# Twenty-one transposes of a fused attention and MLP kernel taken from TensorE to a trip of 32 by 32 blocks through DRAM and VectorE

## The chip, the cores and the metric

The kernel runs on one core of a Trainium2 chip. The metric is device microseconds of one execution; the time before is the median of three. An execution has five instruction streams: TensorE (PE, with its weight loads shown apart as PEld), VectorE (DVE), ScalarE (ACT), GpSimd (POOL) and SyncE (SP). In this kernel SP issues every DMA, in the order of the program. Each engine works off its own stream in order, and a semaphore holds an instruction until what it reads is there.

## The reference, cut to what matters

The input is `x`, four sequences of 512 tokens with 512 features, all float32. A gated linear attention and then an MLP with 4-bit weights are each added to the residual:

```python
x = x + attention(layernorm(x))
x = x + down(gelu(gate(layernorm(x))) * up(layernorm(x)))
```

The attention works by head (4 of 128 features) and by chunk (4 of 128 tokens in each sequence):

```python
q, k, v = h @ Wq + bq, h @ Wk + bk, h @ Wv + bv       # h = layernorm(x)
k = k / max(norm(k), 1e-12)
scores = (q @ k.T) * beta.T * decay                    # within a chunk, causal
y = scores @ v + (q @ state) * chunk_decay
state = state * total_decay + v.T @ (k * beta * decay_to_end)
```

A product on TensorE contracts over partitions. So `h`, which is computed with tokens on partitions, has to be turned until features lie on partitions before it can be multiplied with a weight, and `k` has to be turned the same way before `q @ k.T`.

## The kernel before, in words

**Units of work.** A norm tile is 128 tokens of one sequence with all 512 features; sequence `b` has four, `n` = 0 to 3. Its turned form goes into `hT[b]`, two tiles of 128 partitions. A chunk `(b, n)` is the attention of 128 tokens of sequence `b`.

**Steps.** The kernel is recorded by hand (`manual_schedule`), so each engine's order is the order in which the Python code issues. The main loop counts steps `p`; sequence `b` has the twelve steps 12b to 12b+11: four products `product_v` (L375, L382), four `product_q` (L400), four `product_k` (L412). After each product `behind(p)` issues the rest of the step. The chunks of sequence `b` run nine steps behind: chunk `(b, n)` takes the three steps from p = 9 + 12b + 3n. A period here is such three steps:

- `p % 3 == 0`: `chunk_lead` (L519) turns `k` by four transposes on TensorE, and ScalarE copies the result into `kT` (L522). `chunk_decay` makes the decay `dm` on ScalarE (L534) and GpSimd (L538).
- `p % 3 == 1`: `turn("f")` transposes the MLP's norm tile (L333, `tp_f`). ScalarE rounds it to `g` (L356), VectorE forms two more parts (L357, L358), and three DMAs store them (L360). `turn("a")` transposes the attention's next norm tile (L333, `tp_a`), and ScalarE copies it to `hT` in two parts (L348). Then `chunk_scores`: TensorE forms `sp` (L586), and VectorE multiplies it into `dm` (L597).
- `p % 3 == 2`: `chunk_sums`: TensorE forms `dp` (L611) and `yp`, which reads `dm` (L640, L642). VectorE adds `yp` to the residual `xr` (L649), and SP stores it (L650). Then `second_norm` takes the statistics of `xr`, `first_norm` those of the next sequence's tile (L298 to L305), and `settle` normalises both (L312: first `hn_f`, then `hn_a`).

So from one `yp` on VectorE to the next there is a cycle: `xr`, both norms, `settle`, then the `g` parts and `dm`, then the next `yp`.

**When norm tiles come.** `early` in the code sets it: sequence 1 at p = 2, 5, 8 and 8; sequence 2 at p = 11, 14, 17, 20; sequence 3 at p = 23, 26, 29, 32. Sequence 0 is turned at the start.

**Other work in the same streams.** At `j` = 3 to 7 of each sequence the gates are computed: `gates_ln` (p % 12 == 5) is a chain of small VectorE operations with two ScalarE logarithms in the middle (L467 to L482). Unpacking of MLP weights is slipped in between (L162 to L183), and `fetch` issues the loads of the next weights (L196, L201 for `gu`, six DMAs; L215, L217 for `d`, two DMAs). Loads of the MLP's first inputs (L283, `x<-h`) begin at p = 40.

**Buffers.** Tiles of 2 KB per partition come from a list of 42 free places (`one_k`), PSUM from eight banks in turn. DMAs use eight semaphores in turn, so a DMA waits until the one issued eight places earlier has landed.

Of the kernel before, what the change touches and what calls it, by code (L numbers as in the profile page):

```python
# [8 lines left out]
F32 = mybir.dt.float32  # L9
# [4 lines left out]
AF = mybir.ActivationFunctionType  # L14
ALU = mybir.AluOpType
# [6 lines left out]
P = 128  # L22
# [13 lines left out]
def f32(t):  # L36
    return t.bitcast(F32)
# [3 lines left out]
def tile_gated_linear_attention__then__nvfp4_geglu(  # L41
# [19 lines left out]
    nc = tc.nc  # L61
    B, T, D = x.shape
    H = D // P
    NCH = T // P
    NT = B * NCH
    KC = D // P
# [8 lines left out]
    dram = ctx.enter_context(tc.tile_pool(name="dram", bufs=1, space=DRAM))  # L75
# [45 lines left out]
    one_k = Homes("b", 42, [P, T], two_k)  # L121

    def psum(name):
        return fps.tile([P, T], F32, tag="p", name=name)

    def heads(t):
        return t.rearrange("p (h d) -> p h d", d=P)

    def bc(a):
        return a.unsqueeze(2).to_broadcast([P, a.shape[1], P])  # L130
# [144 lines left out]
    acc, hT, q_sb, k_sb, v_sb = {}, {}, {}, {}, {}  # L275
# [5 lines left out]
    def load(src, name):  # L281
        t = one_k.get(name)
        nc.sync.dma_start(f32(t), src)  # L283
        return t
# [7 lines left out]

    settled, turned = [], []

    def norm(src, key, use, parts=1, within=None):

        st = small.tile([P, 6], F32, tag="st", name=f"st_{key}")
        nc.vector.bn_stats(st, f32(src))  # L298
        if within:
            within()  # L300
        mv = small.tile([P, 2], F32, tag="mv", name=f"mv_{key}")
        nc.vector.bn_aggr(mv, st)
        rs = small.tile([P, 1], F32, tag="rs", name=f"rs_{key}")
        nc.vector.tensor_scalar(rs, mv[:, 1:2], 1e-5, None, ALU.add)
        nc.gpsimd.tensor_tensor(rs, rs, minus_half[:, :1], ALU.pow)  # L305

        def settle():

            hn = one_k.get(f"hn_{key}")
            w = D // parts  # L310
            for cols in (slice(i * w, (i + 1) * w) for i in range(parts)):
                nc.vector.tensor_scalar(  # L312
                    f32(hn)[:, cols].rearrange("p (c two j) -> p c two j", two=2, j=P),
                    f32(src)[:, cols].rearrange("p (c j two) -> p c two j", two=2, j=P),
                    mv[:, 0:1], rs, ALU.subtract, ALU.mult,
                )
            one_k.put(src)
            turned.append((hn, key, use))

        settled.append(settle)  # L320
# [6 lines left out]
    def turn(which, most=NT):  # L327
        for done in [t for t in turned if t[1][0] in which][:most]:
            turned.remove(done)
            hn, key, use = done  # L330
            tp = psum(f"tp_{key}")
            for k in range(KC):
                nc.tensor.transpose(tp[:, k * P : (k + 1) * P], f32(hn)[:, k * P : (k + 1) * P], ident)  # L333
            one_k.put(hn)
            use(tp)

    def first_norm(b, n, src, within=None):
        if n == 0:
            hT[b] = [two_k.get(f"hT{b}_{c}") for c in range(KC // 2)]

        soon = b == n == 0

        def use(tp):
            for c in range(KC // 2):
                to = f32(hT[b][c])[:, :, n * P : (n + 1) * P]
                new = tp[:, 2 * c * P : 2 * (c + 1) * P].rearrange("p (two t) -> p two t", two=2)
                for part in ((0, 1), (1, 2)) if soon else ((0, 2),):
                    nc.scalar.copy(to[:, slice(*part), :], new[:, slice(*part), :])  # L348

        norm(src, f"a{b}_{n}", use, 2 if soon else 1, within)  # L350

    def second_norm(b, n, src):
        def use(tp):
# [40 lines left out]
    def product_q(b, h):  # L394
# [10 lines left out]
            f32(q_sb[b][h // 2])[:, h % 2, :], pq, AF.Identity, bias=bq_sb[:, h : h + 1]  # L405
        )

    def product_k(b, n):

        pk = psum(f"pk_{b}_{n}")  # L410
        for k in range(KC):
            nc.tensor.matmul(  # L412
                pk, f32(hT[b][k // 2])[:, k % 2, n * P : (n + 1) * P], f32(wk[k // 2])[:, k % 2, :],
                start=(k == 0), stop=(k == KC - 1),
            )
        kt = one_k.get(f"k_{b}_{n}")
        k_sb[b, n] = kt
        nc.vector.tensor_tensor(f32(kt), pk, f32(bk_sb), ALU.add)
        return lambda: k_factors(b, n, kt)

    def k_factors(b, n, kt):
        sq = one_k.get(f"sq_{b}_{n}")
        sn = small.tile([P, H], F32, tag="ss", name=f"ss{b}_{n}")
        for h in range(H):
            hs = slice(h * P, (h + 1) * P)
            nc.scalar.activation(
                f32(sq)[:, hs], f32(kt)[:, hs], AF.Square, accum_out=sn[:, h : h + 1]
            )
        one_k.put(sq)
        nc.gpsimd.tensor_scalar(sn, sn, 1e-24, None, ALU.max)  # L430
        nc.gpsimd.tensor_tensor(sn, sn, minus_half, ALU.pow)
        brn = small.tile([P, H], F32, tag="brn", name=f"brn{b}_{n}")
        nc.gpsimd.tensor_tensor(brn, sn, beta[b][:, n * H : (n + 1) * H], ALU.mult)
        kwf = small.tile([P, H], F32, tag="kwf", name=f"kwf{b}_{n}")
        nc.gpsimd.tensor_tensor(kwf, sn, bdte[b][:, n * H : (n + 1) * H], ALU.mult)
        ss[b, n] = brn, kwf
# [66 lines left out]
    def gates_end(b):  # L503
        nc.vector.tensor_tensor(bdte[b], bdte[b], beta[b], ALU.mult)
# [8 lines left out]
    state, ch = {}, {}  # L513

    def chunk_lead(b, n):
        kT = one_k.get(f"kT_{b}_{n}")
        tp = psum(f"tpk_{b}_{n}")
        for h in range(H):
            nc.tensor.transpose(  # L519
                tp[:, h * P : (h + 1) * P], f32(k_sb[b, n])[:, h * P : (h + 1) * P], ident  # L520
            )
        nc.scalar.copy(f32(kT), tp)  # L522
        ch["kT"] = kT
# [38 lines left out]
    def chunk_values(b, n):  # L562

        brn, kwf = ss.pop((b, n))
        kt = k_sb[b, n]
        if n + 1 < NCH:
            kw = one_k.get(f"kw_{b}_{n}")
            nc.gpsimd.tensor_tensor(heads(f32(kw)), heads(f32(kt)), bc(kwf), ALU.mult)
            ch["kw"] = kw
        vb = one_k.get(f"vb_{b}_{n}")  # L570
        ch["vb"] = vb
        if b < B - 1:
            nc.gpsimd.tensor_tensor(heads(f32(vb)), heads(f32(v_sb[b, n])), bc(brn), ALU.mult)
        else:
            for h in range(H):
                hs = slice(h * P, (h + 1) * P)
                nc.scalar.activation(
                    f32(vb)[:, hs], f32(v_sb[b, n])[:, hs], AF.Copy, scale=brn[:, h : h + 1]
                )
# [83 lines left out]
    for b in range(1, B):  # L663
        for n in range(NCH):
            p = 3 * NCH * (b - 1) + 3 * n - 1 if b > 1 else 2 + 3 * min(n, 2)
# [5 lines left out]
    def chunk_of(p):  # L671
        b, n = divmod((p - 2 * NCH - 1) // 3, NCH)
        return (b, n) if 0 <= b < B else None
# [24 lines left out]
    def behind(p):  # L698
        place[0] = p + 1
        b, j = divmod(p, 3 * NCH)  # L700
        chunk = chunk_of(p)
        first = b < B
        if not first:
            between_steps(p)
        left = chunk if p not in met else None
        if p % 3 == 0:
            if left:
                chunk_lead(*chunk)
            exps = gates_exp(b) if first and j == 3 else None
            if chunk and chunk[1] == 0:  # L710
                chunk_values(*chunk)
            if first and j == 6:
                exps = gates_sums(b)
            if left:
                chunk_decay(*chunk)
            if exps:
                exps()
        elif p % 3 == 1:
            turn("f")

            if p > 1:
                turn("a")
            if left:
                chunk_scores(*chunk)
            if first and j == 7:
                gates_end(b)
                load_sums(b, 0)
            for t in early.get(p + 4, ()):
                if t[0] > 1:
                    xs[t] = load(tile_of(t[0] * NCH + t[1]), f"x{t[0]}_{t[1]}")  # L730
            t = (p - 2 * NCH - 2) // 3 + 1
            if 0 <= t < NT:
                acc[divmod(t, NCH)] = load(tile_of(t), f"xr{t}")
        else:
            if first and j == 5:
                gates_ln(b)
            if chunk and not summed:
                sums, rest = chunk_sums(*chunk)
                sums()
                summed.append(rest)  # L740
            while summed:
                summed.pop()()
            for t in early.get(p, ()):
                first_norm(*t, xs.pop(t))
            if p + 1 < 3 * NCH * B:
                settle()
# [173 lines left out]
    with tc.manual_schedule():  # L920
# [3 lines left out]
        bv_sb, bk_sb = one_k.get("bv"), one_k.get("bk")  # L924
# [40 lines left out]
        blocks = mlp()  # L965
        p = 0
# [95 lines left out]
```

## Time and profile before

| | |
|---|---|
| median of three runs | 1308.07 us (1307.88 to 1308.34) |
| profiled execution, its own time | 1308.09 us |
| its span, from first to last instruction | 1306.1 us |
| the time around the span | 1.99 us |
| granted TensorE clock | 0.999 |

| stage, us from the span's start | PE busy | DVE busy | ACT busy | DMA share |
|---|---|---|---|---|
| 8.0 to 34.5 | 26.50 | 10.63 | 6.39 | 0.51 |
| 34.5 to 57.0 | 22.50 | 7.94 | 10.93 | 0.35 |
| 57.0 to 117.0 (steps 12 to 23) | 60.00 | 38.80 | 25.21 | 0.44 |
| 117.0 to 177.0 (steps 24 to 35) | 60.00 | 41.04 | 25.85 | 0.45 |
| 177.0 to 237.0 (from step 36) | 60.00 | 35.83 | 26.47 | 0.55 |
| 237.0 to 280.0 | 40.32 | 34.37 | 28.50 | 0.96 |
| 280.0 to 330.0 | 50.00 | 41.38 | 18.03 | 0.77 |

The page of a profile gives the share of busy time by engine, the chain of work that ended last (followed back from the end, with its share by engine and line) and groups of equal instructions with the mean time of one. The trace behind it can be asked for the chain in order of time, for a timeline of one engine, for the waits of one engine, and for the traffic in a short window. In a timeline the columns are start, duration, engine, line, operation and tiles; "SPq" rows are DMA issues, and their duration is the time that SP takes to issue.

### The profile page before, as it was taken

The page shows a single profiled execution, that of the slowest core. Times are in us where ns is not written, and L with a number is a line of the kernel's source. Part 1 is how long each engine was busy: PE and PEld are TensorE (multiplying, and loading weights), DVE is VectorE, ACT ScalarE, POOL GpSimd, SP SyncE. Part 2 cuts the span into 40 slices and gives each one's busy share as a digit, 9 for nine tenths or more (in the row PEclk, how much of TensorE's full clock was granted, in tenths as well). Part 3 has the DMA queues.
Part 4 walks back from the last instruction along what each step waited for, and adds up shares of the span by engine and source line. Part 5 has one row for each costly group of instructions (what it writes and reads, how often), then busy time and mean ns, then how long its engine had stood idle before and what let it go on. Part 6 is the DMA issues. An engine that isn't in the chain of part 4 may idle for free.

```text
span 1306.1 us, 17024 instructions
## 1 busy us (share of the span) xinstructions
PE 1296.4 (99%) x5808; PEld 1038.3 (79%) x5808; DVE 954.0 (73%) x1539; ACT 461.5 (35%) x908; POOL 108.9 (8%) x179
## 2 busy tenths in 40 slices
PE   9999999999999999999999999999999999999998
PEld 6677676778888888888888888888888888887886
DVE  3467665798777777777777777777777777777566
ACT  2443435753333333333333333333333333332332
POOL 1535263410000000000000000000000000000000
PEclk9999999999999999999999999999999999999999
DMA  5235446888555555555555555555555555555463
GB/s 194 82 108 173 123 128 211 266 272 261 184 184 187 187 185 183 187 186 184 185 186 186 186 187 184 186 184 187 183 186 186 188 183 186 185 177 197 169 248 128
DMA packets 176374, 240.79 MB, mean 184 GB/s; under 512 B 16096, under 2 KB 74784, under 8 KB 176288
## 3 DMA queue, kind: packets, MB, share of 16 engines
q1 hardware_dynamic: 176288, 239.72, 56.7%
q8 instruction: 45, 0.74, 0.2%
q14 instruction: 41, 0.34, 0.1%
HBM read 187.19 MB, written 52.46 MB: 183 GB/s over the span
## 4 chain that ended last, share of the span: by engine, by line
PE 96%; DMA 2%; DVE 2%; ACT 1%; issue 0%; SPq 0%; POOL 0%; DVEq 0%; ACTq 0%; POOLq 0%
PE pa L774 35%; PE p_d L818 26%; PE pb L774 17%; PE pq L400 4%; PE pk L412 4%; PE pva L375 2%; PE pvb L382 2%; PE sp L586 1%; PE yp L640 1%; PE dp L611 1%; DMA x<-h 1%; PE yp L642 1%; PE tp_a L333 1%; PE tp_f L333 0%; PE tpk L519 0%; DMA h<-g 0%
## 5 line engine op out<-in xcount | busy, mean ns | idle before, releaser
L774 PE MATMUL pa<-x,wgu 128*128 128x512 f32 x2048 | 507.1, 390 | 0.0
L774 PEld LDWEIGHTS pa<-x,wgu 128*128 128x128 f32 x2048 | 383.9, 188 | 79.0
L818 PE MATMUL p_d<-wd,i 128*128 128x512 f32 x1542 | 357.3, 390 | 2.3 <-DVE xr L649 0.6
L818 PEld LDWEIGHTS p_d<-wd,i 128*128 128x128 f32 x1542 | 288.4, 188 | 65.7 <-DVE i L798 2.1
L779 ACT ACTIVATE t<-pb 128x512 f32<-128x512 f32 x256 | 151.2, 591 | 358.9 <-PE pb L774 355.5
L774 PE MATMUL pb<-x,wgu 128*128 128x512 f32 x1024 | 275.3, 390 | 1.5 <-DMA x<-h 1.4
L780 DVE TENSOR_TENSOR t<-pa,t 128x512 f32<-128x512 f32 x256 | 176.5, 690 | 82.6 <-ACT t L779 76.9
L774 PEld LDWEIGHTS pb<-x,wgu 128*128 128x128 f32 x1024 | 192.3, 188 | 43.0 <-DMA x<-h 3.2
L826 DVE SCALAR_TENSOR_TENSOR acc<-p_d,acc 128x512 f32<-128x512 f32 (+1 forms) x137 | 93.4, 682 | 124.4 <-PE p_d L818 123.9
L794 ACT ACTIVATE i<-t 128x512 fp32r<-128x512 f32 x128 | 81.0, 633 | 194.2 <-DVE t L791 191.2
L786 ACT ACTIVATE t<-t 128x512 f32<-128x512 f32 x128 | 81.1, 634 | 135.8 <-DVE t L780 135.7
L798 DVE TENSOR_TENSOR i<-t,i 128x512 fp32r<-128x512 f32 x128 | 88.4, 690 | 25.9 <-ACT i L794 24.1
L830 DVE TENSOR_TENSOR acc<-acc,p_d 128x512 f32<-128x512 f32 x135 | 92.9, 688 | 14.1
L791 DVE SCALAR_TENSOR_TENSOR t<-t,t 128x512 f32<-128x512 f32 x128 | 88.6, 692 | 4.3
L799 DVE SCALAR_TENSOR_TENSOR i<-i,t 128x512 fp32r<-128x512 f32 x128 | 88.1, 689 | 0.0
L849 POOL TENSOR_TENSOR acc<-acc,last 128x512 f32<-128x512 f32 x1 | 1.3, 1295 | 1015.1 <-ACT last L848 1015.1
L400 PE MATMUL pq<-hT,wq 128*128 128x512 f32 x128 | 57.7, 595 | 0.0
L412 PE MATMUL pk<-wk,hT 128*128 128x512 f32 x128 | 57.4, 593 | 0.0
L400 PEld LDWEIGHTS pq<-hT,wq 128*128 128x128 f32 x128 | 23.3, 191 | 23.5 <-issue 23.4
L412 PEld LDWEIGHTS pk<-wk,hT 128*128 128x128 f32 x128 | 23.2, 191 | 23.4 <-issue 23.4
L183 DVE TENSOR_TENSOR wgu<-wgu,wgu 128x1024 fp32r<-128x1024 f32 x32 | 39.0, 1218 | 0.0
L171 DVE SCALAR_TENSOR_TENSOR w_gu<-i_gu,sc_gu 128x1024 f32<-128x1024 f16 x32 | 38.9, 1216 | 0.0
(117 smaller groups left out, 913.7 us busy)
## 6 DMA issues: line engine op xcount, KB each, us to landing
x<-h SPq DMA_DIRECT2D x420, 256.0 KB
acc<-acc SPq DMA_DIRECT2D x256, 256.0 KB
h<-g SPq DMA_DIRECT2D x48, 256.0 KB
x<-in_x SPq DMA_DIRECT2D x16, 256.0 KB
pk_gu<-in_gate_p SPq DMA_DIRECT2D x32, 128.0 KB
sc_gu<-in_gate_s SPq DMA_DIRECT2D x64, 64.0 KB
pk_gu<-in_up_p SPq DMA_DIRECT2D x32, 128.0 KB
sc_gu<-in_up_s SPq DMA_DIRECT2D x64, 64.0 KB
```

What stands on the lines that cost most here:

```text
L400: nc.tensor.matmul(pq, f32(wq[k // 2])[:, k % 2, h * P : (h + 1) * P], f32(hT[b][k // 2])[:, k % 2, :], start=(k == 0), stop=(k == KC - 1),)
L412: nc.tensor.matmul(pk, f32(hT[b][k // 2])[:, k % 2, n * P : (n + 1) * P], f32(wk[k // 2])[:, k % 2, :], start=(k == 0), stop=(k == KC - 1),)
L774: nc.tensor.matmul(o, w3[j][:, k % 2, c * P : (c + 1) * P], x[j * KC + k], start=(j == js[0] and k == 0), stop=(j == js[-1] and k == KC - 1),)
L779: nc.scalar.activation(f32(t), pb, AF.Copy, scale=-1.0 / ONE_E)
L780: nc.vector.tensor_tensor(f32(t), pa, f32(t), ALU.add)
L786: nc.scalar.activation(f32(g), f32(g), AF.Gelu_apprx_tanh, scale=ONE_E)
L791: nc.vector.scalar_tensor_tensor(f32(u), f32(g), ONE_E, f32(u), ALU.mult, ALU.mult)
L798: nc.vector.tensor_tensor(il, f32(u), f32(ih), ALU.subtract)
L799: nc.vector.scalar_tensor_tensor(im, f32(ih), ONE_E, f32(u), ALU.mult, ALU.subtract)
L818: nc.tensor.matmul(banks[key_][:, part], inter[i][j][:, n * P : (n + 1) * P], wd[ms[i] // 2][j][:, ms[i] % 2, part], start=(i == 0 and j i ...
L826: nc.vector.scalar_tensor_tensor(a, banks[n, False, part.start][:, part], ONE_E, a, ALU.mult, ALU.add)
L830: nc.vector.tensor_tensor(a, a, banks[n, True, 0], ALU.subtract)
```

## The change

Two kinds of tiles are no longer transposed on TensorE: the twelve norm tiles of sequences 1 to 3, and the nine `k` tiles with `0 < n` and `b < 3`. The function `far` names the latter.

Such a tile is written by VectorE in another column order (`crossed`), stored by one DMA of 256 KB into DRAM (`cross`), and loaded back by four DMAs of 64 KB (`land`), so that the 32 by 32 blocks stand in their turned places. VectorE then transposes within the blocks (`turn_blocks`): two instructions of 128x256 elements for a norm tile, one of 128x512 for a `k` tile. They write `hT` and `kT` directly; the ScalarE copies are gone.

Places in the order: the store of a norm tile is issued in `settle`, at the end of its step; its loads at the next `p % 3 == 0`, and the VectorE transposes at the next `p % 3 == 1`, ahead of `turn("f")`. The store of a `k` tile is issued in `product_k`; its loads at the step before its chunk begins, and its VectorE transpose in `chunk_lead`. The normalisation of a norm tile becomes two instructions of 256 columns in place of one of 512. The readers and the writer of a `k` tile in the new order (L418, L426, L568) get access patterns with one more dimension. TensorE, ScalarE and GpSimd keep the order of everything else.

```diff
+    def cross(src, key, use):
+        way = dram.tile([KC, P, P], F32, tag=f"way_{key}", name=f"way_{key}")
+        nc.sync.dma_start(way.rearrange("w p m -> p w m"), f32(src).rearrange("p (w m) -> p w m", m=P))
+        return way, key, use
+
+    def land(way, key, use):
+        t = one_k.get(f"way_{key}")
+        for a in range(KC):
+            nc.sync.dma_start(f32(t)[:, a * P : (a + 1) * P], way[:, a * 32 : (a + 1) * 32, :])
+        return lambda: use(t)
+
+    def turn_blocks(t, *to):
+        new = f32(t).rearrange("p (a k i) -> p k a i", a=KC, i=32)
+        done = 0
+        for part in to:
+            n = part.shape[1]
+            nc.vector.transpose(part.rearrange("p k (a j) -> p k a j", j=32), new[:, done : done + n])
+            done += n
+        one_k.put(t)
...
         def settle():
             hn = one_k.get(f"hn_{key}")
+            if way:
+                for c in range(2):
+                    nc.vector.tensor_scalar(
+                        crossed(f32(hn)).rearrange("p (c two) w i -> p c two w i", c=2)[:, c],
+                        f32(src).rearrange("p (c w i two) -> p c two w i", c=2, w=KC, two=2)[:, c],
+                        mv[:, 0:1], rs, ALU.subtract, ALU.mult,
+                    )
+                one_k.put(src)
+                coming.append(cross(hn, key, way))
+                one_k.put(hn)
+                return
...
-        norm(src, f"a{b}_{n}", use, 2 if soon else 1, within)
+        def way(t):
+            turn_blocks(t, *(f32(hT[b][c])[:, :, n * P : (n + 1) * P] for c in range(KC // 2)))
+
+        norm(src, f"a{b}_{n}", use, 2 if soon else 1, within, way if b > 0 else None)
...
+    def far(b, n):
+        return 0 < n and b < B - 1
...
-        nc.vector.tensor_tensor(f32(kt), pk, f32(bk_sb), ALU.add)
+        nc.vector.tensor_tensor(heads_of(kt, far(b, n)), in_blocks(pk), in_blocks(f32(bk_sb)), ALU.add)
+        if far(b, n):
+            ways[b, n] = cross(kt, f"k{b}_{n}", lambda t: turn_blocks(t, heads(f32(ch["kT"]))))
...
     def chunk_lead(b, n):
+        if far(b, n):
+            ch["kT"] = one_k.get(f"kT_{b}_{n}")
+            ways.pop((b, n))()
+            return
...
         if p % 3 == 0:
+            come.extend(land(*t) for t in coming)
+            coming.clear()
             if left:
                 chunk_lead(*chunk)
...
         elif p % 3 == 1:
+            while come:
+                come.pop(0)()
             turn("f")
...
         else:
+            after = chunk_of(p + 1)
+            if after and far(*after):
+                ways[after] = land(*ways[after])
```

More of the change, by code (lines that the diff above doesn't have):

```diff
@@ L293, in tile_gated_linear_attention__then__nvfp4_geglu, with crossed, norm @@
     settled, turned = [], []
-    def norm(src, key, use, parts=1, within=None):
+    coming, come = [], []
+    def crossed(t):
+        return t.rearrange("p (w k i) -> p k w i", w=KC, i=32)
+    def cross(src, key, use):
[15 more added lines that the diff above has]
+        one_k.put(t)
+    def norm(src, key, use, parts=1, within=None, way=None):
         st = small.tile([P, 6], F32, tag="st", name=f"st_{key}")
@@ L406, in product_q, with in_blocks, heads_of @@
         )
+    def far(b, n):
+        return 0 < n and b < B - 1
+    ways = {}
+    def in_blocks(a):
+        return a.rearrange("p (h w i) -> p h w i", h=H, i=32)
+    def heads_of(t, blocks):
+        return crossed(f32(t)) if blocks else in_blocks(f32(t))
     def product_k(b, n):
@@ L426, in k_factors @@
             nc.scalar.activation(
-                f32(sq)[:, hs], f32(kt)[:, hs], AF.Square, accum_out=sn[:, h : h + 1]
+                f32(sq)[:, hs].rearrange("p (w i) -> p w i", i=32), heads_of(kt, far(b, n))[:, h],
+                AF.Square, accum_out=sn[:, h : h + 1],
             )
@@ L567, in chunk_values @@
             kw = one_k.get(f"kw_{b}_{n}")
-            nc.gpsimd.tensor_tensor(heads(f32(kw)), heads(f32(kt)), bc(kwf), ALU.mult)
+            nc.gpsimd.tensor_tensor(
+                in_blocks(f32(kw)), heads_of(kt, far(b, n)),
+                kwf.unsqueeze(2).unsqueeze(3).to_broadcast([P, H, KC, 32]), ALU.mult,
+            )
             ch["kw"] = kw
```

## The prediction, made before the changed kernel was run

> **What bounds the kernel now.** I read the engine shares first, then the chain, then the chain in order of time. The page gives TensorE as the limit, and nearly the whole chain is TensorE:
>
> ```profile
> PE 1296.4 (99%) x5808; PEld 1038.3 (79%) x5808; DVE 954.0 (73%) x1539; ACT 461.5 (35%) x908; POOL 108.9 (8%) x179
> ...
> PE 96%; DMA 2%; DVE 2%; ACT 1%; issue 0%; SPq 0%; POOL 0%; DVEq 0%; ACTq 0%; POOLq 0%
> ```
>
> The chain in order of time (start, us, what) shows no gap between TensorE's pieces around a period of chunk (0,1). Four transposes take 0.44 us each time, so each group taken away shortens the chain by that, if nothing else becomes late:
>
> ```profile
> 60.01 0.44 PE tpk L519 x4
> 60.45 1.78 PE pva L375 x8
> 62.23 1.73 PE pvb L382 x8
> 63.95 0.44 PE tp_f L333 x4
> 64.39 0.44 PE tp_a L333 x4
> 64.83 0.89 PE sp L586 x8
> ```
>
> Next, what could become late: VectorE's timeline, in the cycle from one `yp` to the next. TensorE ends a `yp` at 71.91 (next piece of the chain: `pva` at 71.91).
>
> ```profile
> 71.94 0.69 DVE L649 TENSOR_TENSOR xr<-xr,yp 128x512 f32<-128x512 f32 x1 [2.19 <-PE yp L642]
> ...
> 76.27 0.55 DVE L312 TENSOR_SCALAR hn_a<-x,mv_a,rs_a 128x512 f32<-128x512 f32 x1 [0.44 <-POOL rs_a L305]
> ...
> 80.53 0.69 DVE L357 TENSOR_TENSOR g<-tp_f,g 128x512 fp32r<-128x512 f32 x1 [2.01 <-ACT g L356]
> 81.14 0.68 DVE L358 SCALAR_TENSOR_TENSOR g<-g,tp_f 128x512 fp32r<-128x512 f32 x1
> 81.74 0.68 DVE L597 TENSOR_TENSOR dm<-sp,dm 128x512 f32<-128x512 f32 x1
> ```
>
> `dm` is done at 82.42 and the next `yp` starts at 85.38 (dp at 84.49 plus 0.89): a slack of 3.0 us. It covers whatever holds VectorE up between `hn_a` and `dm`.
>
> Last, what a DMA takes. SP issues an 8 KB store and then a load that needs it:
>
> ```profile
> 34.82 0.36 SPq L492 DMA_DIRECT2D rows<-rows  x1
> 36.21 0.35 SPq L508 DMA_DIRECT2D sums<-rows  x1
> ```
>
> That is 1.39 us from issue to the dependent issue. The 256 KB store issued at 88.43 moves bytes from 89.2 to 90.0, by short windows:
>
> ```profile
> 89.20:89.40 0.20, 0.20 (x2) 0.15 (x1) 0.17 (x2) 0.00 (x0) 0.00 (x0) 1.00 0.63 236
> ...
> 89.80:90.00 0.20, 0.20 (x1) 0.00 (x0) 0.20 (x1) 0.00 (x0) 0.20 (x1) 1.00 0.75 277
> ```
>
> **What goes.** Twelve groups `tp_a` and nine `tpk`: 21 x 0.437 (the spacing 64.39 to 64.83 and its like) = 9.2 us of TensorE, all on the chain: 1.75 before 57 us, 3.07 in each of the two stages of 60 us, 1.3 after 177. ScalarE's copies go too (24 x 0.38 + 9 x 0.58 = 14 us); it is half idle, so I price that at nothing.
>
> [...]
>
> **What comes, off the path.** VectorE: settling in two instructions instead of one (0.41 us for 128x256 in sequence 0's first tile, against 0.55 for 512) adds 0.2; two transposes of 256 columns, not shown in the trace, lie between 0.66 (two at 0.33, the spacing that 0.41 us instructions keep) and 1.3 (two at 0.69, as a 512-column one), and I take 0.8, nearer the row of equal size. For `k` one of 0.7. In all 12 x 1.0 + 9 x 0.7 = 18 us on an engine that has 21 us idle of 60. The new patterns on L418, L426 and L568 I take as unchanged: below nothing is excluded as the work is the same; were GpSimd's `kw` twice its 1.04 us, its 32 us of idle time per 60 cover it. DMA: 21 x 512 KB = 10.75 MB at a share of 0.35 to 0.55.
>
> The `k` trips have room. Store and loads are two steps apart or more, and loads are issued 3.4 us or more before VectorE reaches the transpose. Price 0, but for the last, below.
>
> **What comes on the path: the norm tile's trip.** Where VectorE meets `turn_blocks` before the data is there it stands, and behind it stand both `g` parts, `dm` and so `yp`. Counted from the end of `yp` (Y):
>
> - `hn_a` ends at Y+4.9 (76.82), 0.2 later now; store issued at Y+5.15.
> - The store: 1.39, less its 0.2 of traffic, plus 0.8, plus 0.2 for an issue of 0.56 (three `h<-g` of this shape take 1.70) = 2.2. SP issues the loads at Y+7.35, held by the store's landing.
> - Four loads: three issues of 0.53 ahead of the last (between 0.33 for `x` and 0.64 for `sc_gu`), and 1.8 for the last to land. No lone 64 KB load is shown: 1.39 (8 KB) is the lower end, 2.71 (the first 256 KB load of `x`, 0.79 to 3.50) the upper; 64 KB is nearer the former. Together 3.4: Y+10.75. VectorE has stood since about Y+7.6.
> - Transposes 0.8, `g` parts 1.2, `dm` 0.7: done at Y+13.45.
>
> TensorE wants `yp` at Y + three products (3.51 for v, 3.44 for q or k) + tp_f 0.44 + sp 0.89 + dp 0.89 = 12.75, or 12.54 with q and k alone. So it waits 0.7 to 0.9 per period, about what the period saves (0.88).
>
> [...]
>
> The eight periods, by their settling step:
>
> - p = 11: 0.7. p = 14: 0.85. p = 23: 0.7.
> - p = 17 and 29: `gates_ln` has run between `dm` and `xr`. Its chain needs 3.1 + 0.75 us of VectorE from `dm`'s start (81.74 to 84.86; 86.97 to 87.71), so `xr` starts at Y+16.65, 1.4 after `yp` ends (15.25). `rps` and `cps` give TensorE 0.86 more. 13.45 + 1.4 - 13.4 = 1.4 each.
> - p = 20: no state update (0.55 less), but the loads stand behind the `k` store, which waits for the next `k` on VectorE (Y+6.4): loads from Y+7.0, wait 0.6. p = 32: the same, and two weight loads ahead: 1.0.
> - p = 26: six weight loads stand between store and loads (3.6 us, 133.26 to 136.85), so the loads leave at 9.3 and share the engines: 2.35 later, 3.2.
>
> Sum 9.85. **Sequence 1's tiles.** At p = 5 the first weights' six loads, which now run ahead to 14.5 us, come to stand between store (35.85) and loads (40.0). VectorE stands to 43.4, and `k_0_0` is added at 44.3 instead of 42.24. The tiles of p = 8 settle 2.1 to 2.4 later; their eight loads land at 53.6 and 55.7; `dm` is done at 57.2, where TensorE wants it at 53.86 (55.61 - 1.75): 3.3. **The last `k` tile**: its loads stand behind six `x<-h` loads (206.81 to 211.10), landing about 214.6, VectorE done at 215.3, `sp` wanted at 215.0 less little: 0.6.
>
> **Sum.** -9.2 + 9.85 + 3.3 + 0.6 = +4.6 on the profiled 1308.09, which is the median (1308.07) within 0.02: 1312.6, and with semaphore hops I say 1313. The stages after 237 us keep their length; there TensorE idles only 2.7 of 43 us.
>
> **Rivals.**
> - *The trip is covered*: all 9.2 us are kept, 1298.9. It decides where store and loads take under 4.7 us (12.6 less 2.7 of VectorE work less 5.15) instead of 5.6. For it: 1.39 us for the 8 KB store, 3.0 us of slack. Against: four issues and two landings. With loads at their lower ends (3 x 0.33 + 1.39 = 2.4) the waits fall by 1.0 per period to 3.5, sequence 1's to 1.6, the last to 0: 1304.
> - *The trip is slower*: loads at the upper ends (3 x 0.64 + 2.7 = 4.6) and transposes of 1.3: 1.7 more in each of eight periods and 3 at the other places, 1329.
> - *Break-even*: half a microsecond off each trip: 1308, within the measurement.
> - *TensorE's time does not fall*: excluded by the order, in which exactly these 21 groups are missing and nothing else moves.
>
> **Numbers.** Forecast (1311 to 1320) 0.48; slower trip (to 1329) 0.18; break-even 0.13; partly covered, around 1304, 0.13; fully covered 0.08. The range reaches from 1302 to 1327. About 0.2% (2.6 us) is what a measurement here can tell from no change. Faster 0.21, same 0.13, slower 0.66.
>
> **What would show it.** Right: TensorE waits at L640 for `dm`, 0.5 to 1.5 us in each of eight periods, VectorE idle ahead of the 128x2x128 transposes released by DMA `way`, steps 12 to 35 longer than 120 us, the p = 26 and p = 8 tiles worst. Wrong: VectorE reaching the transposes after the data, or TensorE waiting for `hT` or `kT`.

## The result, and the profile after

The changed kernel takes 1371.59 us (median of four, 1368.55 to 1376.23), beside 1308.20 for the kernel before (1307.88 to 1310.53): 1.0484 times as long, 95% interval 1.0449 to 1.0518. The forecast was 1313 with a range to 1327, so the sign was right and the size far off. The profiled execution took 1376.23 us, its span 1374.5 against 1306.1: 68.4 us more.

The page of the changed kernel, busy time by engine, the granted TensorE clock in 40 slices, and the chain's share by engine:

```profile
PE 1312.7 (96%) x5724; PEld 1046.4 (76%) x5724; DVE 971.0 (71%) x1584; ACT 450.4 (33%) x875; POOL 111.6 (8%) x179
...
PEclk9888999999999999999999999999999999999999
...
PE 79%; DMA 8%; DVE 5%; issue 2%; SPq 2%; POOL 1%; ACT 1%; DVEq 0%; POOLq 0%; ACTq 0%
```

TensorE has 84 instructions fewer and yet is busy 16.3 us longer, DMA has gone from 2% to 8% of the chain, and in slices 2 to 4 the clock, never below 9 before, is at 8. What TensorE waits for (us in total, times, longest):

```profile
PE yp L706 <- DVE dm L663: 37.6, 9, 7.2
PE sp L652 <- DVE ncla L555: 7.0, 1, 7.0
PE tpk L582 <- DVE k L474: 5.3, 1, 5.3
```

The first row is the wait that the prediction named, in the number of places that it named, but 4.2 us each instead of about one. The second is the last `k` tile (`ncla` is a small gate tile that VectorE makes right behind `kT` there), the third the first `k` of sequence 0, which VectorE forms behind one of sequence 1's tiles. VectorE in turn waits for the trip:

```profile
DVE hT L320 <- DMA way_a<-way_a: 80.3, 12, 12.1
```

**Where the 68.4 us lie.** Sixteen times, once a chunk, VectorE adds `yp` to `xr`. The start of that instruction (L649 before, L715 after) marks the same point of the work in both traces, so the differences between its starts are a budget by place that needs no guess about causes. The other columns are experiments told below; the numbers are what each place takes beyond the kernel before, in us, in the profiled executions.

| place, by starts of `xr` | before | after | e1 | e3 | e4 | e8 | e10 | e13 |
|---|---|---|---|---|---|---|---|---|
| up to the first (sequence 1's tiles) | 56.54 | +14.6 | +5.3 | +4.4 | -0.6 | +12.4 | -1.9 | -0.3 |
| first to ninth (eight periods with a norm tile) | 120.44 | +41.7 | +15.9 | +4.6 | -1.6 | +39.1 | +4.7 | -3.5 |
| ninth to twelfth (the last `k` tile) | 44.62 | +9.7 | +5.4 | +5.4 | +8.5 | +11.3 | 0.0 | 0.0 |
| twelfth to sixteenth | 59.49 | +2.6 | +2.5 | -0.3 | +3.2 | +2.9 | -0.2 | +2.7 |
| rest of the span | 1025.0 | -0.2 | -0.2 | -0.2 | -0.1 | -0.1 | -0.1 | -0.1 |

**One regular period.** The chain in order of time of the changed kernel, in the first of the eight (its `xr` starts at Y = 71.12, 0.03 us after `yp` ends; start, us, what):

```profile
76.21 2.29 DMA way_a<-hn_a
...
80.25 5.23 DMA way_a<-way_a
...
86.37 0.58 DVE g L401
86.95 0.59 DVE g L402
87.54 0.61 DVE dm L663
...
88.20 0.49 PE yp L706 x2
```

Against the prediction's own steps: store at Y+5.09 (forecast 5.15), landed after 2.29 us (2.2), loads from Y+7.39 (7.35), `dm` done 2.67 us after the landing (2.7). Only one step is off: from the issue of the last load to its landing it took 5.23 us where the forecast had 1.8. So `yp` starts at Y+17.08 and the period lasts 19.9 us (the next `xr` starts at 91.01) instead of 15.4.

While almost nothing but these loads is on the queues, the short windows of the changed kernel (stretch, length, PE busy, clock, share of the 16 DMA engines, GB/s) show

```profile
80.50:81.00 0.50, 0.50 (x4) 1.00 0.29 88
81.00:81.50 0.50, 0.50 (x4) 1.00 0.27 81
```

0.27 to 0.29 of 16 engines is four to five engines' worth. Each load reads `way[:, a*32:(a+1)*32, :]`, a pattern of 4 x 32 x 128 whose slowest dimension is 4. That the 4 and the four to five engines belong together is the author's estimate from these two rows; the views show only the mean share of the 16. For the loads the prediction took the size of a DMA as its price and did not look at its shape.

### The profile page after: what moved, and what is told of

Same layout as the page of the kernel before. It is cut to its first block, busy times and chain, and to the rows that moved or that the text cites. A ratio compares the mean times of both kernels' runs of the same rounds, so it can differ in the third digit from the quotient of the medians.

```text
span 1374.5 us, 17026 instructions
## 1 busy us (share of the span) xinstructions
PE 1312.7 (96%) x5724; PEld 1046.4 (76%) x5724; DVE 971.0 (71%) x1584; ACT 450.4 (33%) x875; POOL 111.6 (8%) x179
## 2 busy tenths in 40 slices
DMA packets 198551, 251.81 MB, mean 183 GB/s; under 512 B 16768, under 2 KB 96960, under 8 KB 198464
## 4 chain that ended last, share of the span: by engine, by line
PE 79%; DMA 8%; DVE 5%; issue 2%; SPq 2%; POOL 1%; ACT 1%; DVEq 0%; POOLq 0%; ACTq 0%
PE pa L847 33%; PE p_d L891 24%; PE pb L847 16%; DMA way_a<-way_a 4%; PE pk L468 2%; DMA x<-h 2%; SPq L311 1%; DMA way_a<-hn_a 1%; PE yp L706 1%; PE yp L708 1%; SPq L201 1%; PE pva L419 1%; DMA way_k<-way_k 1%; POOL rs_a L335 0%; DVE hT L320 0%
## 5 line engine op out<-in xcount | busy, mean ns | idle before, releaser
L903 DVE TENSOR_TENSOR acc<-acc,p_d 128x512 f32<-128x512 f32 x135 | 92.8, 687 | 14.1
L320 DVE STREAM_TRANSPOSE hT<-way_a 128x256 f32<-128x256 f32 x24 | 9.3, 424 | 80.3 <-DMA way_a<-way_a 80.3
L706 PE MATMUL yp<-vb,dm 128*128 128x128 f32 x128 | 29.2, 333 | 37.6 <-DVE dm L663 37.6
L468 PE MATMUL pk<-wk,hT 128*128 128x512 f32 x128 | 61.7, 629 | 0.0
L706 PEld LDWEIGHTS yp<-vb,dm 128*128 128x128 f32 x128 | 23.5, 236 | 41.5 <-DVE dm L663 40.9
```

Source lines behind the costliest of these rows:

```text
L468: nc.tensor.matmul(pk, f32(hT[b][k // 2])[:, k % 2, n * P : (n + 1) * P], f32(wk[k // 2])[:, k % 2, :], start=(k == 0), stop=(k == KC - 1),)
L903: nc.vector.tensor_tensor(a, a, banks[n, True, 0], ALU.subtract)
```

## The experiments

Theory A, after the result, an estimate from the share of 0.27 to 0.29: the loads by column groups run on four engines, all four loads on the same ones, and that is the missing 3.4 us of each trip. Rival B: the data was written to DRAM a moment before, and reading it back costs a turnaround, whatever the shape. A third question was how much of the loss is TensorE's clock: the span grew by 52.1 us of idle TensorE, by 25.5 us of busy time beyond what its work explains (16.3 + 9.2), less the 9.2 us removed.

### e1: the same bytes in loads by rows

```diff
-        for a in range(KC):
-            nc.sync.dma_start(f32(t)[:, a * P : (a + 1) * P], way[:, a * 32 : (a + 1) * 32, :])
+        for w in range(KC):
+            nc.sync.dma_start(
+                f32(t)[w * 32 : (w + 1) * 32, :].rearrange("j (a m) -> j a m", m=P),
+                way[w].rearrange("(a j) m -> j a m", j=32),
+            )
```

> The four loads of a trip are cut by groups of 32 partitions instead of by groups of 128 columns; bytes, number of DMAs and places in the order stay. Theory A (the column-group loads keep only four of the sixteen DMA engines busy: in the changed kernel's trace the share is 0.27 to 0.29 from 80.5 to 81.5 us, where only they run): the wait from the last issue to landing falls from about 5.2 us to about 2, the waits of TensorE at yp fall from 37.6 us to under 15, the granted clock returns to above 0.99, and the time lies between 1300 and 1322 us. Theory B (a load that follows a store of the same DRAM bytes is slow however it is cut): the landing stays at 4.5 us or more and the time above 1355 us.

1335.50 us (1330.98 to 1336.71), ratio 1.0180 [1.0158, 1.0202]: 36 us of the 63 are gone (38, if each kernel is set against the times of the kernel before beside it). In the chain of this run the last load of a regular period lands in

```profile
70.56 1.90 DMA way_a<-way_a
```

after a store of 2.29 us, and `yp` starts at Y+13.34, where the forecast had 13.45. While these loads run, a short window (columns as above) shows a larger share of the engines at work than 0.27 to 0.29:

```profile
70.50:71.00 0.50, 0.50 (x5) 1.00 0.43 124
```

B falls: the same data, as freshly written, lands in 1.90 instead of 5.23 us. Nor is it the number of packets, which hardly differs (198551 in the change, 199559 here). A's forecast holds for the landing (about 2 us, measured 1.90), but the time is 13.5 us above its upper end; that it was four engines remains an estimate. The waits for `dm` in this run say that the other periods still lose:

```profile
PE yp L709 <- DVE dm L666: 17.2, 8, 4.0
```

One of the eight, 4.0 us, is sequence 1's (forecast 3.3); the eight periods wait 13.1 us in the other seven, where the forecast's sum was 9.85. Period by period, the three regular ones (p = 11, 14, 23) wait 0, 0.4 and 0.8 us and the two with `gates_ln` 2.0 and 1.0, about as forecast (though at p = 14 and 23 `dm` is ready only at Y+14.1 and Y+14.7, and the wait is short because TensorE itself had stood 1.0 us for `kT`). The rest stands where SP's queue has something else around the store and the loads. The store of p = 20, issued behind six weight loads, takes 5.25 us to land, and the loads leave at Y+9.8 instead of 7.0 (wait 2.7); those of p = 26 stand behind six weight loads, and VectorE has the data at Y+15.7 instead of 13.1 or so (wait 4.0).

So in e1's eight periods TensorE idles 16.7 us: 13.1 for `dm` and 3.5 for `kT`, which the forecast had at nothing. It is busy 5.3 us longer than its work at full clock would take. Less the 6.1 us of work removed (14 groups), this is the table's 15.9.

### e2 and e3: VectorE's transposes behind `g` and `dm`

```diff
-            while come:
-                come.pop(0)()
             turn("f")
...
             if left:
                 chunk_scores(*chunk)
+            while come:
+                come.pop(0)()
```

e2 has this edit on the changed kernel, e3 has it and e1's.

> The loads stay by columns; VectorE's transposes of the norm tiles are issued behind the g parts and dm instead of ahead of them. If the loss comes through the place (VectorE stands with g and dm behind it), TensorE's wait for dm all but goes: the trip lands about 13.8 us after yp, when VectorE has done dm and xr is not due before 14.4: 1300 to 1325 us. If the wait only moves (VectorE then stands ahead of xr and the norms, and the cycle is as long), the time stays above 1345 us.

> Both edits together. If trip and place are the whole loss, what is left is the 9.2 us of TensorE time less a few small waits (the weight loads between store and loads at p = 5, the last k tile): 1297 to 1304 us, below the kernel before. If something else also costs (VectorE's added 18 us, DMA traffic, the copies through DRAM), it stays at 1306 us or more.

e2: 1356.40 us (1352.26 to 1357.19), ratio 1.0339 [1.0319, 1.0359]. The wait of `yp` is gone, and stands elsewhere:

```profile
PE sp L652 <- DVE kT L320: 15.2, 5, 4.3
PE sp L652 <- DVE ncla L555: 11.9, 3, 6.6
PE tp_f L374 <- DVE hn_f L353: 8.4, 3, 4.0
```

VectorE takes its instructions in order, so whatever is put behind a wait is late: first `dm` (37.6 us of waits in the change), now the next `kT` and `hn_f` (15.2 and 8.4 us here). Moving a wait by one place saved 15 us, not the wait. e3: 1322.96 us (1320.77 to 1324.41), ratio 1.0089 [1.0072, 1.0107], better than both and still slower than before.

### e4 and e5: each half alone

e4 leaves only the nine `k` tiles on the trip, e5 only the twelve norm tiles.

> Only the nine k tiles take the trip; all norm tiles are turned by TensorE as in the kernel before. By the prediction's pricing the k trips have room but for the last: 9 x 0.437 = 3.9 us less of TensorE and one wait of up to 1 us, 1304 to 1307 us. In the changed kernel VectorE waits 12.0 us for k tiles, 9.8 of it at one; if that is the k trips' own doing and reaches TensorE, the time is above 1312 us.

> The change with the norm tiles' trip alone; the nine k tiles are turned by TensorE as before. If the two halves of the change only add up, this is what the whole change loses (63.4 us) less what the k tiles' half lost alone (5.1 us): about 58 us over the kernel before, 1362 to 1372. If the halves lean on each other (stores and loads of k tiles standing on SP's queue ahead of those of the norm tiles, VectorE with the work of both), it is clearly below: 1335 to 1355.

e4: 1315.54 us (1312.87 to 1317.31), ratio 1.0035 [1.0025, 1.0045]; e5: 1364.41 us (1359.68 to 1364.88), ratio 1.0429 [1.0411, 1.0446]. The losses, 5.1 and 55.9 us, add up to 61 of the change's 63, so the halves do not need each other. By the table, the six `k` tiles between e4's first and ninth `xr` save 1.6 us, and the three after them lose 8.5 together. It is the last one, whose loads stand on SP's queue behind six `x<-h` loads; its fourth load waits for one of them to land (chain in order of time of e4):

```profile
204.32 7.21 DMA x<-h
...
211.55 6.27 DMA way_k<-way_k
```

After them VectorE turned `kT` at 217.94, and TensorE had stood 6.7 us. The forecast named this place and gave it 0.6.

### e8: the clock

```diff
+        if ch.pop("fill", None):
+            fill = psum(f"fill_{b}_{n}")
+            for i in range(14):
+                nc.tensor.matmul(fill[:, :P], ident, ident, start=True, stop=True)
         yp = psum(f"yp_{b}_{n}")
...
         elif p % 3 == 1:
+            if come:
+                ch["fill"] = True
```

It adds matmuls inside TensorE's waits; their result is read by nobody.

> The change as it is, with 14 matmuls of the identity more (128x128, 0.22 us each, 3.1 us together, their result unused) on TensorE just ahead of the yp matmuls of each period that has a norm tile's transposes, that is inside the waits of 3.6 to 7.2 us. If the 25 us by which TensorE's busy time exceeds its work are half-clock stretches that the idle gaps bring on, the gaps now stay under some 1.5 us for most periods, the granted clock goes back to 0.99 or more, and the time falls by 15 to 25 us, to 1347 to 1357, though TensorE does some 35 us more. If the clock follows something else (DMA or VectorE traffic in this stage), the time stays at 1369 to 1376 and the clock near 0.98.

First what they are meant to prevent. In the changed kernel TensorE idles from 84.5 to 88.2 us; short windows behind that gap (columns as above):

```profile
88.00:89.00 1.00, 0.80 (x7) 1.00 1.03 288
89.00:90.00 1.00, 1.00 (x9) 0.67 1.00 237
90.00:91.00 1.00, 1.00 (x6) 0.50 0.97 355
91.00:92.00 1.00, 1.00 (x3) 0.50 0.45 165
```

The first matmuls run at full clock; from about 89.3 on, one microsecond after the work resumed, the clock is half, until about 92.7, and the `pva` group there takes 2.92 us instead of 1.95. Such stretches are what the 25.5 us are made of: a mean clock of 0.94 up to 57 us, 0.89 from there to 237 and 0.95 to 300 is some 26 us of full clock missing. With the filling, the same stretch of its period has

```profile
89.00:90.00 1.00, 1.00 (x6) 1.00 0.64 223
90.00:91.00 1.00, 1.00 (x6) 1.00 0.58 199
```

The clock is back (granted 0.991 over the run, 0.99 instead of 0.89 between 57 and 237 us). TensorE still waits 15.0 us for `dm` in nine places. And the time has not changed by more than the runs spread: 1371.41 us (1367.03 to 1373.38), beside 1371.59 for the change. The expectation of 15 to 25 us is refuted. The cycle from one `yp` to the next goes through `xr`, the norm, the trip, VectorE and `dm`; TensorE's products of the same period run beside it, and most of the half-clock stretches lie in their slack.

Not all of them: `yp` itself is on the cycle. Here is the fifth of the eight periods, without the filling and then with it (rows of TensorE's and of VectorE's timeline):

```profile
166.59 0.80 PE L706 MATMUL yp<-vb,dm 128*128 128x128 f32 x2 [4.24 <-DVE dm L663]
170.41 0.69 DVE L715 TENSOR_TENSOR xr<-xr,yp 128x512 f32<-128x512 f32 x1 [2.48 <-PE yp L708]
```

```profile
164.50 0.49 PE L710 MATMUL yp<-vb,dm 128*128 128x128 f32 x2 [1.09 <-DVE dm L663]
166.59 0.69 DVE L719 TENSOR_TENSOR xr<-xr,yp 128x512 f32<-128x512 f32 x1 [0.74 <-PE yp L712]
```

From the start of `yp` to the next `xr` it is 3.82 us at half clock and 2.09 at full clock. Over the eight periods these stretches take 23.6 us in the change and 17.7 with the filling, so 5.9 us of the slow clock lay on the cycle. Of these, 3.3 are lost again between `xr` and `yp`, 2.2 of them at p = 20, where the tile's store takes 4.27 us with the filling and its loads leave at Y+8.8 instead of Y+6.8. What is left is the table's difference: the eight periods cost 39.1 us more than before with the clock restored, 41.7 without. So most of the first budget, 52 us of idling and 25 of slow clock, was bookkeeping: both are filled by the same late `dm`.

### e6 and e7: every known place repaired

On top of e1 and e3: a norm tile's VectorE transposes are put off by one period, the `k` loads are issued one step sooner (ahead of the `x<-h` loads), and the first fetch of weights goes from behind step 5 to behind step 6 (behind sequence 1's loads). e7 is the same with the loads by columns.

```diff
-            come.extend(land(*t) for t in coming)
+            come.extend((p, land(*t)) for t in coming)
...
         elif p % 3 == 1:
-            while come:
-                come.pop(0)()
             turn("f")
...
+            after = chunk_of(p + 2)
+            if after and far(*after):
+                ways[after] = land(*ways[after])
             if left:
                 chunk_scores(*chunk)
+            while come and come[0][0] < p - 3:
+                come.pop(0)[1]()
...
         else:
-            after = chunk_of(p + 1)
-            if after and far(*after):
-                ways[after] = land(*ways[after])
...
-                if p in (5, 7):
+                if p in (6, 7):
```

> The whole change with its loads cut by rows, VectorE's transposes of a norm tile put off by one period of three steps (so that some 15 us more lie between the tile's store and its use), the k tiles' loads issued one step sooner (ahead of the six x<-h loads that the last k tile stood behind) and the first fetch of weights moved from behind step 5 to behind step 6 (behind sequence 1's loads, not ahead of them). Theory 'only the trip's length at a place that waits for it': nothing waits any more, TensorE does 9.2 us less and keeps its full clock, 1299 to 1304. Rival 'the extra work on SP, VectorE and GpSimd costs by itself, wherever it stands' (the run with both cures was still 13 us over the kernel before): 1310 to 1320, with waits of TensorE for VectorE that have no DMA behind them.

> The same as the run beside it, but with the loads by column groups as in the change (last issue to landing 4.5 to 5.2 us instead of 1.9). If the slow loads cost only where something waits for them, the time is that of the run beside it within 3 us. If loads that go to a few of the engines also hold up the other transfers (x, weights, sums), 5 to 15 us more than the run beside it, with waits for other DMAs in the list.

e6: 1312.02 us (1310.40 to 1315.45), ratio 1.0025 [1.0015, 1.0034]: in the rival's range, but without the rival's sign. From 117 to 237 us TensorE idles under 2 us in all; one large stall is left, 62 to 69 us, and it has a DMA behind it: the last load of sequence 0's first travelling `k` tile lands at 64.4. e7: 1326.97 us, ratio 1.0146 [1.0131, 1.0161], 15 us above e6. That is the size of the second expectation, but not its sign: no other DMA appears in the list of TensorE's waits. Instead `sp` waits 17.7 us for `kT` in five places, and VectorE 19.9 us for the `k` tiles' loads in four: their lead is too little for slow loads.

### e9 to e12: which places are left

e9 is e6 without the trip of that first `k` tile, e10 is e6 without any `k` tile, e11 is e9 with the norm tiles' loads by columns, and e12 is the kernel before with the moved fetch alone.

> The repaired change (rows, norm tiles' transposes a period later, k loads a step sooner, fetch behind step 6) less the trip of one k tile, tile 1 of sequence 0, which TensorE turns as before. In the repaired run TensorE stood 3.3 us for that tile from 62.1 us on, idled again to 69 and ran at half clock from about 65 to 72. If those waits and the half clock behind them are what the repaired run still loses, 6 to 8 us go: 1303 to 1306, faster than the kernel before. If the half clock is only slack that another wait takes up (as the filled run showed for the change itself), only the 3.3 us of the wait goes: 1308 to 1310, no different from the kernel before.

> The same without any k tile on the trip: the norm tiles' twelve alone, by rows and a period late. TensorE does 12 x 0.437 = 5.2 us less. If the norm tiles' trip costs nothing once it has a period's time, 1302 to 1305. If the stores and loads on SP's queue or the 0.77 us of VectorE in each period still cost something, 1307 to 1312.

> As the first run of this call, but the norm tiles' loads by column groups as in the change (landing 4.5 to 5.2 us behind the last issue), the k tiles' by rows. If a slow load costs only where its result is waited for, the first run's time within 2 us. If loads on a few engines delay what else is on the queues, 4 us or more above it, and TensorE's waits name k tiles, x or sums.

> The kernel before with only the first fetch of weights moved from behind step 5 to behind step 6. It is a control: if a repaired version beats the kernel before, this tells whether the moved fetch alone does so. Expected 1307 to 1309, no difference.

e9: 1310.88 us (1308.70 to 1313.47), ratio 1.0016 [1.0006, 1.0025]; e10: 1310.16 us (1308.69 to 1312.24), ratio 1.0007 [0.9999, 1.0016]. Both miss the better of their expectations (e9 lies 0.9 us above the other one, too), and in both the stall has only changed its name. TensorE's waits in e10, and a piece of its chain:

```profile
PE pva L422 <- DVE hT L323: 5.7, 1, 5.7
```

```profile
46.89 8.13 DMA way_a<-hn_a
...
69.09 3.89 PE pva L422 x8
```

The stores of sequence 1's last two tiles, issued behind eight loads of weights among others, take 8.1 us instead of 2.3. SP holds eight loads for them, and the loads of `sums` and `xr` after those; ScalarE's decay waits for `sums`, and VectorE reaches the two tiles at 68.6 us. The first period of e10 is 7.8 us longer than before: the wait of 5.7, and 2.5 more because the next products are on the chain here and run slow behind the wait (`pva` 3.89 us for 1.78, `pvb` 2.09 for 1.73; the granted clock is 0.94 from 57 to 117 us, where it was 1.00 before), less one group. Its other seven take 101.99 us where the kernel before takes 105.04: 3.05 less, which is seven groups of 0.436. So where nobody waits for the trip, it does give what it removes.

e11: 1316.62 us (1311.97 to 1318.58), ratio 1.0046 [1.0029, 1.0062], 5.7 us above e9. That is in the range of the second expectation, loads that delay what else is on the queues, but it is not explained: the runs lie at 1312 to 1313 and at 1317 to 1319, and the profiled one (1311.97) is of the lower three. In its trace TensorE's waits have the names of e9's, 0.7 us more for `hT` and 0.9 more for `kT`; VectorE waits 4.5 us for `k` tiles, which it does not in e9, and ScalarE 41.3 us for `sums` where e9 has 28.9. What slow loads cost in the slower runs stays open. e12: 1308.08 us, ratio 0.9996 [0.9987, 1.0005]: the moved fetch alone does nothing.

### e13 and e14: without sequence 1

Only sequences 2 and 3 travel, by rows and with the transposes a period later; the fetch is back behind step 5. e13 has their eight norm tiles, e14 also the six `k` tiles of sequences 1 and 2.

```diff
-        norm(src, f"a{b}_{n}", use, 2 if soon else 1, within, way if b > 0 else None)
+        norm(src, f"a{b}_{n}", use, 2 if soon else 1, within, way if b > 1 else None)
...
-        return 0 < n and b < B - 1
+        return False
```

In e14 the last line returns `0 < n and 0 < b < B - 1`.

> Only the norm tiles of sequences 2 and 3 travel (8 tiles, by rows, transposes a period later); sequence 1's and all k tiles are turned by TensorE, the fetch is behind step 5 as before. TensorE does 8 x 0.437 = 3.5 us less. If a trip that nobody waits for is free, 1304 to 1306, ratio 0.996 to 0.998. If the added work of SP and VectorE costs by itself, 1308 to 1312.

> The same with the six k tiles of sequences 1 and 2 travelling too (by rows, loads a step sooner): 14 x 0.437 = 6.1 us less of TensorE, and VectorE 6 x 0.2 us more that may stand in front of scores. If free, 1301 to 1304; in the run with these k tiles and sequence 1's norm tiles TensorE waited 2.8 us for k tiles in three places, which would leave 1304 to 1307. If the added work costs, 1309 to 1314.

e13: 1306.09 us (1302.98 to 1307.44), ratio 0.9975 [0.9966, 0.9985]; e14: 1306.23 us (1303.51 to 1307.67), ratio 0.9976 [0.9966, 0.9985]. Both beat the kernel before, e13 by 2.5 us where eight groups are worth 3.5. The table shows the eight periods at -3.5 exactly, and a loss of 2.7 behind the twelfth `xr`, where TensorE waits for `x<-h`; whether the trip causes that one, the runs do not tell. The page of e13 shows 32 TensorE instructions fewer than before, 2.4 us less of busy time, and the 99% of before:

```profile
PE 1294.0 (99%) x5776; PEld 1035.5 (79%) x5776; DVE 960.5 (74%) x1563; ACT 457.1 (35%) x892; POOL 108.4 (8%) x179
```

e14's `k` tiles bring nothing more: 2.6 us less work, and waits of 1.8 us for `kT` and 0.7 for `dm` in its list.

## Why the prediction was wrong, point by point

- **TensorE's 9.2 us.** Right: 0.436 a group, shown for norm tiles by e10's seven periods and e13's eight, and for `k` tiles by e14, which takes 1.3 us off between the ninth and the twelfth `xr`, where it moves three. One transpose is thus worth 109 ns.
- **Store, settling, VectorE.** Right in the regular period: 2.29 us for 2.2, Y+5.09 for Y+5.15, two transposes of 128x256 at 0.424 us each (0.77 with their overlap) for 0.8, one of 128x512 at 0.70 for 0.7.
- **"1.8 for the last to land": the failed step.** It took 5.23 us in the period shown. The term came from loads of whole tiles, and its upper end of 2.71 was the cost of four times the bytes, which seemed safe. With e1's loads the term is 1.90 and the period is as forecast. From the issue of the store to the last landing the trip took 9.3 us, and 5.5 with e1's loads, where the forecast had 5.6 (2.2 and 3.4). In the budget, e1 takes back 25.8 of the eight periods' 41.7 us, and 39.5 of the span's 68.4.
- **"Price 0" for the `k` trips, "0.6" for the last.** In e1 TensorE waits 3.5 us for `kT` in the eight periods. Where the last one stands, between the ninth and the twelfth `xr`, e4 loses 8.5 us: an `x<-h` load took 7.21 us to land, and the last `k` load, which waited for it, 6.27 more.
- **"3.3" for sequence 1.** Up to the first `xr`, the forecast's 3.3 less 1.75 of saved work gives +1.55; measured +14.6, and +5.3 with loads by rows. The place was named rightly. In the change the loads at p = 5, behind six weight loads, landed 6.06 us after the last issue, and the stores at p = 8 took 4.12 us (8.1 in e10) where 2.2 was assumed.
- **p = 20, 26 and 32.** Their order on SP's queue was read rightly, the prices were low: in e1 the waits are 2.7, 4.0 and 2.3 us where 0.6, 3.2 and 1.0 stood.
- **The clock** was not priced. It fell to 0.89 between 57 and 237 us, and e8 shows that most of this lies in slack. The sum lacked a smaller term: where a long gap stands ahead of `yp`, `yp` itself ran at half clock, which stretched the eight periods by 5.9 us beside the run with filling. It follows from the gaps, and so from the failed step: behind the gap of 3.7 us in the period shown the clock was 0.50, and with the gaps filled it was 0.99 between 57 and 237 us.
- **The rivals.** "Trip is slower" had the right mechanism, and too near an end. "The trip is covered" did not happen, but e13 reaches its condition, a trip that nothing waits for, with a period's time and loads by rows.

Put together: the range was too narrow because every load's upper end was taken from transfers of another shape. A regular norm trip then ran 3.6 us beyond its forecast (Y+17.08 for 13.45), at a place where VectorE, working in order, passes the delay on to all that follows. The 25 us that e1 still loses are not explained by that step. By the rows above they lie at the stores and loads that meet weights on the queues, at the `k` tiles priced at nothing or 0.6, and in the slow clock behind the waits; what the 2.5 us behind the twelfth `xr` are stays open.

## What to carry to other kernels

Price a DMA by its access patterns, not by its bytes alone: here the last of four loads of the same bytes landed after 5.23 us with 4 as the slowest dimension of its read and after 1.90 with 32. A result that comes back over DRAM belongs at a point that the in-order engines reach a full period later (e10's seven periods then kept the whole saving, 3.05 us); moving the wait past a few instructions mostly renames it (in e2 it saved 15 us of 63). And before a lost clock is given a price, ask which of TensorE's instructions are on the cycle that sets the period.

## What the runs showed of the hardware that was not expected

- Four 64 KB loads with an outer dimension of 4 landed 4.4 to 5.2 us after the last issue in six of the eight periods, with 0.27 to 0.29 of the DMA engines busy while almost nothing else was on the queues (80.5 to 81.5 us); the same bytes with 32 rows outermost landed in 1.9 us.
- After a gap of 3.7 us TensorE ran about one microsecond at full clock and then some 3.4 us at half. 3.3 us of small matmuls in the gap kept the clock at 1.00 there, and the time stayed within the runs' spread (1371.41 us beside 1371.59).
- A VectorE transpose of 32 by 32 blocks costs what a plain pass costs here: 0.424 us for 128x256 and 0.70 us for 128x512 of float32, where `hn_a` of 128x256 took 0.41 and `xr` of 128x512 took 0.69 in the kernel before.
- A 256 KB store landed in 2.3 us alone and in 4.1 to 8.1 us behind loads of weights that were issued ahead of it (4.12 in the change, 5.25 in e1, 8.13 in e10).
